# Layer 1's GLU spread to the end of the layer, with its buffers kept, and the routing's tables in weight buffers

## The chip, the cores and the metric

The kernel runs on one core of a Trainium2 chip. The metric is the device time of one execution in microseconds (us), the median of several runs. TensorE (PE) does the matmuls, VectorE (DVE) and ScalarE (ACT) the elementwise work, GpSimd (POOL) gathers and some elementwise work, and SyncE (SP) issues most of the DMAs. All of them run their own instruction queue in order and wait for each other by semaphores.

## The reference, cut to what matters

Four layers work on a residual stream `x` of 4 sequences of 512 tokens, width 256, all in float32. In each layer a normalized copy `xn` goes through an attention-like part and a feed-forward part, and both results are added to `x`:

```python
xn = layernorm(x)
x = x + attn_i(xn) + ffn_i(xn)
```

Layer 0 is a Mamba-2 mixer with a GLU. Layer 1 is the layer that the change touches first:

```python
# attention with low-rank queries and keys (16 heads, causal), 512 tokens a sequence
q  = rmsnorm(x @ wq_a) @ wq_b          # 192 -> 16 heads of 128 + 64 (rotary)
kv = rmsnorm((x @ wkv_a)[:, :64]) @ wkv_b
out = softmax(q k^T * scale, causal) v @ wo
# feed-forward: a GLU of width 1024, plus product-key experts
mlp = silu(x @ gate_w) * (x @ up_w) @ down_w
experts = sum over 8 of 512 experts, chosen by two top-8 searches, of silu(x . down_e) * softmax * up_e
```

Layer 2 has a small head-mixing attention, and a feed-forward part with 8 experts of which each token takes the best 2, plus a shared GLU of width 256:

```python
scores = softmax(x @ gate_w)                      # 2048 tokens x 8 experts
topk_w, topk_i = top_k(scores, 2)
y = sum over the 2 of w_e * (silu(x @ wg_e) * (x @ wu_e)) @ wd_e
shared = silu(x @ sg) * (x @ su) @ sd
```

Layer 3 has a full attention of 16 heads and 8 experts with a top-p rule.

## The kernel before

**Tiling.** Tokens are split into 16 tiles of 128 and 4 sequences of 512. `x` (tokens on partitions) and `xnT` (the normalized stream, transposed) stay in SBUF. When every stream of a layer has added its part for a sequence b, `part_done(b)` calls `layernorm(b)` for the next layer, which also writes the normalized tokens to DRAM.

**Weaving.** Inside a layer several Python generators ("streams") issue their work in turn. `weave` gives each stream a total cost and a start, and always advances the one whose place, start plus work done over its total, is lowest:

```python
live = [[start * total, total, gen] for gen, total, start in streams]
s = min(live, key=lambda s: s[0] / s[1])
cost = next(s[2], None)
```

The totals only set how far a stream spreads over the layer: a stream with a total above the sum of its costs ends early. This order is handed to a planner, which places the instructions on each engine's queue and assigns the buffers of each pool. Buffers of one tag are handed out in the order of the program. A pool that is opened over the memory of a closed one waits until all tiles there are done with.

**Layer 1's streams** (`layer1`, lines 1073 to 1104):

- `latent_pieces`: the attention, for 4 groups of 4 heads, 4 sequences and 2 pairs of heads: 32 pairs. For each head, score products (line 655), row maximum on DVE (658), exponential on ACT (662), scaling (775), transposes on PE (782) with copies out (786); for each pair of heads the value product (918, result `zT`), for each two pairs the output product (932) which is added to `x` (158). Queries (739 to 742) are made one pair ahead; half of their rows are turned by a copy from SBUF to SBUF on SP's queue (`psw`, 747). Each group takes a new weight block (713, 714, 721).
- `product_key_pieces`: two searches, then for each of the 16 token tiles 8 gathers on POOL (1036), 8 dot products on DVE (1046) and 8 additions (152).
- `glu_units`: the GLU in two halves of 512 hidden columns. The first half of sequences 0 and 1 is done in layer 0 already. For each half and sequence, four hidden blocks (two projections by line 134 of 512 columns each, tanh on ACT at 165, two DVE operations at 166 and 167, cost 3.4), then two steps of the down product (line 212, two token tiles each, cost 3.44) with an addition to `x` (158).
- `room`: starts at 0.915. It closes the right side's pools, loads layer 2's weights on POOL's queue (1589, 1591) and runs the routing of layer 2 for the first two sequences (`Half.dispatch`): router, softmax, comparison tables `before` and `tie` (1306 to 1310), ranks, counts, places, one-hot tables (1422), and a product of them (1430) that gives the ids of the tokens in each slot of the experts.

**Memory.** Pools with `side="right"` grow from the top of SBUF down, the others from the bottom up. Before, `p_keep`, `p_t` (product keys) and `g1` (the GLU: five `hT` of 2 KB and two `sg` of 2 KB a partition) are on the right, and `room` closes all three to place `t_keep` (25 KB) and `t_route` (14 KB) there. `t_route` holds the routing's tables: `before` in four buffers of 2 KB, and `sel`, `cum`, `pick`, `hit` and small ones. A separate pool `weights` has three buffers of 12 KB with the tag `wu`; every block of weights (`Ctx.unit`) takes the next that is free. In layer 1 the blocks are, in order: the attention's small weights, GLU half 0, attention groups 0 and 1, GLU half 1, attention groups 2 and 3; then layer 2's shared GLU (`t_shared`) and layer 3's four blocks (`f_units`).

**Layer 2** (`Layer2.run`) opens its pools on the right below `t_route`, gathers the tokens for the experts of the first half (`gather`, 1465), runs the second half's routing, the shared GLU, the head mixing and the experts (1495, 1517).

Of the kernel before, what the change touches and what calls it, by code (L numbers as in the profile page):

```python
# [15 lines left out]
P = 128  # L16
# [13 lines left out]
class Ctx:  # L30
# [12 lines left out]
    def tile(self, pool, shape, tag, dtype=F32, **kw):  # L43
        self.n += 1
        return pool.tile(shape, dtype, tag=tag, name=f"{tag}_{self.n}", **kw)
# [37 lines left out]
def v3(ap, b):  # L83
    return ap.rearrange("p (a b) -> p a b", b=b)
# [54 lines left out]
def project_tokens(c, out, w, cols, tokens):  # L139

    for d in range(2):
        c.nc.tensor.matmul(  # L142
            out, lhsT=c.xnT[:, d, tokens], rhs=w[:, d, cols], start=(d == 0), stop=(d == 1)
        )
# [81 lines left out]
def weave(c, *streams, flush=True):  # L226

    live = [[start * total, total, gen] for gen, total, start in streams]  # L230
    while live:
        s = min(live, key=lambda s: s[0] / s[1])
        cost = next(s[2], None)
        if cost is None:
            live.remove(s)
        else:
            s[0] += cost
        c.step()
    if flush:
        c.step(True)  # L240
# [833 lines left out]
def layer1(c, a, xn, following):  # L1074


    with ExitStack() as stack, ExitStack() as right:
        def pool_of(name, bufs, stack=stack, **kw):
            return stack.enter_context(c.tc.tile_pool(name=name, bufs=bufs, **kw))

        p_keep, p_t, glu = (pool_of(name, 1, right, side="right") for name in ("p_keep", "p_t", "g1"))
        dram = pool_of("p_dram", 1, space=bass.MemoryType.DRAM)
        keep = pool_of("l_keep", 1)
        latent = latent_pieces(c, a, keep, lambda: pool_of("l_h", 2))

        def glu_units():
            same = dict(tanh=True, bufs=5)
            yield from glu_pieces(c, glu, [a["g1_units"][0]], last=False, seqs=[2, 3], **same)
            yield from glu_pieces(c, glu, [a["g1_units"][1]], first=1, **same)

        def room():
            right.close()
            following.first()
            yield 1.0
            yield from following.routing(0)

        weave(
            c,
            (latent, 457.0, 0.0),
            (product_key_pieces(c, a, p_keep, p_t, dram, xn), 237.0, 0.02),  # L1100
            (glu_units(), 145.0, 0.0),
            (room(), 270.0, 0.915),
            flush=False,
        )
# [164 lines left out]
def softmax(c, s, m, scale):  # L1269

    nc = c.nc
    wide = list(s.shape)
    nc.vector.tensor_reduce(m, s, AX.X, ALU.max)
    nc.vector.tensor_sub(s, s, m[:, :, None].to_broadcast(wide))
    nc.scalar.activation(s, s, AF.Exp, scale=scale)
    nc.vector.tensor_reduce(m, s, AX.X, ALU.add)
    nc.vector.reciprocal(m, m)
    nc.vector.tensor_mul(s, s, m[:, :, None].to_broadcast(wide))


def router(c, pool, wr, bs, p=None, wide=1):

    nc = c.nc
    E, n = 8, len(bs) * TPB
    pl = c.ps()[:, : n * E]
    for i, b in enumerate(bs):
        c.settle(b)
        for t in range(TPB):  # L1290
            tt, to = b * TPB + t, (i * TPB + t) * E
            project_tokens(
                c, pl[:, to : to + E], wr, slice(0, E), slice(tt * P, (tt + 1) * P)
            )
    yield 2.0
    if p is None:
        p = c.tile(pool, [P, TPB, E], "p")
    nc.vector.tensor_copy(p, v3(pl, E))
    m = c.tile(pool, [P, n], "m")
    softmax(c, p, m, 1.0)  # L1300
    yield 2.0
    full = [P, n, E, E]
    other, own = p[:, :, None, :].to_broadcast(full), p[:, :, :, None].to_broadcast(full)
    before = c.tile(pool, full, "before", bufs=wide)
    tie = c.tile(pool, full, "before" if wide > 1 else "tie", bufs=wide)
    nc.vector.tensor_tensor(before, other, own, ALU.is_gt)
    nc.vector.tensor_tensor(tie, other, own, ALU.is_equal)
    low = v3(c.low, E)[:, None, :, :].to_broadcast(full)
    nc.vector.tensor_mul(tie, tie, low)
    nc.vector.tensor_add(before, before, tie)  # L1310
    return p, m, before, other
# [7 lines left out]
class Half:  # L1319
# [13 lines left out]

    def dispatch(self):
        c, k, pool, nc = self.c, self.k, self.pool, self.c.nc
        tile = lambda shape, tag, **kw: c.tile(pool, shape, tag, **kw)
        p, rank = tile([P, HT, E8], "p_half"), tile([P, HT, E8], "rank")
        before = yield from router(c, pool, k["router"], [2 * self.hf, 2 * self.hf + 1], p, 4)
        yield 2.0
        nc.vector.tensor_reduce(rank, before[2], AX.X, ALU.add)  # L1340

        both = [P, 2, HT, E8]
        sel = tile(both, "sel")
# [4 lines left out]
        cum = tile([P, 4, Z + HT, E8], "cum")  # L1348
# [10 lines left out]
        flat = lambda v: v.rearrange("p t e -> p (t e)")  # L1359
        pc = c.ps()  # L1360
        n = HT * E8
# [10 lines left out]
        full = [P, E8, E8]  # L1372
# [16 lines left out]
        pick = tile(both, "pick")  # L1389
# [11 lines left out]
        hit = tile(by_tile, "hit")  # L1401
# [16 lines left out]
        ats = []  # L1418
        four = [P, 4, P]
        for i in range(2 * HT // 4):  # L1420
            ats.append(tile(four, "before", bufs=4))
            nc.vector.tensor_tensor(
                ats[i], k["iota"][:, None, :].to_broadcast(four),
                part[:, 4 * i : 4 * i + 4][:, :, None].to_broadcast(four), ALU.is_equal,
            )
            yield 1.0
# [203 lines left out]
def top_p_experts(c, a):  # L1630
    nc, tc = c.nc, c.tc
    with tc.tile_pool(name="o_t", bufs=1, side="right") as pool:
        wr = c.tile(pool, [P, 16], "wr")
        nc.sync.dma_start(wr, a["o_router"])
        cws = c.tile(pool, [P, NTILE, 8], "cw")
        for b in range(NB):
            p, _, before, other = yield from router(c, pool, v3(wr, 8), [b])
            nc.vector.tensor_mul(before, before, other)
            cw = cws[:, b * TPB : (b + 1) * TPB, :]
            nc.vector.tensor_reduce(cw, before, AX.X, ALU.add)  # L1640
            nc.vector.scalar_tensor_tensor(
                cw, cw, float(np.float32(0.9)), p, ALU.is_le, ALU.mult
            )
            yield 1.0
        yield from glu_pieces(
            c, pool, [a["o_units"][e] for e in range(8)], factor=lambda e, t: cws[:, t, e : e + 1]
        )
# [17 lines left out]
def program(tc, a, x_in, out):  # L1665
    nc = tc.nc
    with ExitStack() as stack:
# [18 lines left out]
        c.parts(3, lambda b: layernorm(c, b, halves[b // 2][b % 2 * SEQ : (b % 2 + 1) * SEQ, :]))  # L1686
        second = Layer2(c, a, halves)
        layer1(c, a, c.xn, second)
        c.parts(3, lambda b: layernorm(c, b))
        c.pinned = True  # L1690
# [12 lines left out]
def rows(w):  # L1703

    k = w.shape[0] // P
    return w.reshape(k, P, -1).transpose(1, 0, 2).reshape(P, -1)
# [33 lines left out]
def glu_units(gate, up, down):  # L1740

    return np.stack([
        np.concatenate([rows(gate[:, s]), rows(up[:, s]), rows(down[s])], axis=1)
        for s in (slice(k, k + 512) for k in range(0, gate.shape[1], 512))
    ])
# [110 lines left out]
```

## Time and profile before

| what | us |
|---|---|
| median of 5 runs | 3129.32 |
| lowest and highest run | 3127.09, 3137.24 |
| the profiled execution | 3127.98 |
| its span, first to last instruction | 3126.2 |
| TensorE busy in the span | 3073.1 |
| VectorE, ScalarE, GpSimd busy | 1816.7, 1258.1, 650.4 |

All times inside the execution are counted from the start of the span. In the profile a line such as `PE mm L134 x8` names the engine, the tile that is written, the line of the kernel and the number of instructions; a float32 matmul of the program stands there as two instructions. `[3.35 <-PE mm L1430]` behind an instruction is the time that its engine stood before it, and what ended that. Layer 1 begins near 816 us and its attention ends near 1519 us.

### The profile page before, as it was taken

What the parts mean: (1) busy time and instruction counts of PE and PEld (TensorE: products, weight loads), DVE (VectorE), ACT (ScalarE), POOL (GpSimd) and SP (SyncE); (2) the same over time, 40 slices, a digit from 0 to 9 for tenths busy, and PEclk for the clock granted to TensorE, in tenths of its full rate; (3) what the DMA queues carried; (4) which work ended last, traced back from release to release, by engine and by line L of the source; (5) the groups of instructions that cost most, each with busy time, mean ns of one, the idle gap of its engine ahead of it and who ended that gap; (6) DMA issues with size and microseconds to landing.
All of it is one profiled execution on the core that took longest, in us unless ns stands there. A gap on an engine that the chain in (4) does not pass through costs nothing.

```text
span 3126.2 us, 35680 instructions
## 1 busy us (share of the span) xinstructions
PE 3073.1 (98%) x12502; PEld 1885.3 (60%) x12502; DVE 1816.7 (58%) x4644; ACT 1258.1 (40%) x2916; POOL 650.4 (21%) x517
## 2 busy tenths in 40 slices
PE   9999999999899999999999999999999999999999
PEld 5566566566655555555776656656566655555555
DVE  5777778777777787877656545455555422222222
ACT  4434435444466666667425433333333311111111
POOL 0465555556300133331242000000000000000000
PEclk9999999999999999999899999999999999999999
DMA  3233333233221154543242000000000000000000
GB/s 124 86 101 122 100 92 112 85 125 86 89 60 53 45 129 96 130 120 116 67 115 83 1 21 8 1 28 1 21 1 1 21 21 21 21 21 21 0 0 27
DMA packets 89090, 185.12 MB, mean 59 GB/s; under 512 B 14192, under 2 KB 57216, under 8 KB 84176
## 3 DMA queue, kind: packets, MB, share of 16 engines
q1 hardware_dynamic: 74448, 135.05, 13.6%
q0 software_dynamic: 14176, 47.01, 6.5%
q8 instruction: 99, 1.62, 0.2%
q10 hardware_dynamic: 288, 0.79, 0.1%
q14 instruction: 79, 0.65, 0.1%
HBM read 160.92 MB, written 12.98 MB: 56 GB/s over the span
## 4 chain that ended last, share of the span: by engine, by line
PE 88%; DVE 6%; POOL 2%; ACT 2%; DMA 1%; issue 1%; SPq 0%; ACTq 0%; DVEq 0%; POOLq 0%
PE mm L134 34%; PE acc L212 9%; PE mm L655 8%; PE mm L142 5%; PE acc L1165 4%; PE acc L671 4%; PE tr L509 3%; PE tr L1157 2%; PE tr L782 2%; PE tr L212 2%; PE acc L918 2%; PE acc L932 2%; PE acc L488 1%; PE mm L1495 1%; PE mm L478 1%; PE mm L741 1%
## 5 line engine op out<-in xcount | busy, mean ns | idle before, releaser
L134 PE MATMUL mm<-xnT,wu 128*128 128x512 f32 x2128 | 951.6, 595 | 0.2
L134 PEld LDWEIGHTS mm<-xnT,wu 128*128 128x128 f32 x2128 | 400.6, 191 | 462.0 <-issue 438.6
L662 ACT ACTIVATE pr<-pr,nm 128x128 f32<-128x128 f32 (+3 forms) x512 | 285.7, 558 | 293.6 <-DVE nm L658 291.2
L202 DVE TENSOR_TENSOR hT<-sg,mm 128x512 f32<-128x512 f32 x176 | 120.4, 684 | 393.8 <-PE mm L134 388.7
L201 ACT ACTIVATE sg<-mm 128x512 f32<-128x512 f32 x176 | 104.6, 595 | 580.0 <-PE mm L134 579.8
L658 DVE CUSTOM_DVE_ANT_0 pr<-mm,late 128x128 f32<-128x128 f32 (+3 forms) x512 | 245.3, 482 | 92.0 <-PE mm L655 89.4
L212 PE MATMUL acc<-wu,hT 128*128 128x256 f32 x1280 | 287.1, 380 | 1.7 <-DVE x L158 1.7
L212 PEld LDWEIGHTS acc<-wu,hT 128*128 128x128 f32 x1280 | 241.4, 190 | 49.9 <-issue 17.2
L1036 POOL DMA_INDIRECT e<-in_p_experts,ids x128 | 130.4, 1018 | 477.0 <-DVE x L152 354.0
L134 PE MATMUL mm<-xnT,w_in 128*128 128x512 f32 x512 | 228.5, 593 | 0.1
L280 DVE SCALAR_TENSOR_TENSOR cy<-mm,ws,cy 128x509 f32<-128x509 f32 (+2 forms) x216 | 159.7, 745 | 65.4 <-ACT cy L276 61.8
L655 PE MATMUL mm<-kf,qf 128*128 128x128 f32 (+3 forms) x512 | 179.6, 451 | 2.0 <-DVE nm L658 1.3
L655 PE MATMUL mm<-k,q 128*128 128x128 f32 (+3 forms) x512 | 176.5, 434 | 1.0 <-DVE q L1130 1.0
L449 POOL TENSOR_TENSOR G<-G,CB 128x1024 f32<-128x1024 f32 x64 | 152.8, 2388 | 92.5 <-DVE G L415 92.5
L435 ACT ACTIVATE xD<-xc,ws 128x128 f32<-128x128 f32 x256 | 84.1, 391 | 195.9 <-POOL y L472 186.3
L134 PEld LDWEIGHTS mm<-xnT,w_in 128*128 128x128 f32 x512 | 96.7, 190 | 107.9 <-issue 101.2
L152 DVE SCALAR_TENSOR_TENSOR x<-acc,cw,x 128x256 f32<-128x256 f32 x128 | 61.9, 483 | 153.7 <-PE acc L212 153.6
L1165 PE MATMUL acc<-PT,V 128*128 128x512 f32 (+3 forms) x512 | 149.1, 433 | 0.0
L415 DVE TENSOR_TENSOR_SCAN G<-G,eye 128x1024 f32<-128x1024 f32 x64 | 146.8, 2295 | 0.0
L1130 DVE TENSOR_SCALAR q<-mm,bias 128x512 f32<-128x512 f32 x64 | 48.0, 750 | 165.3 <-PE mm L134 165.3
L782 PEld LDWEIGHTS tr<-con,pr 128*128 128x128 f32 x640 | 81.2, 143 | 88.7 <-ACT pr L775 27.4
L142 PE MATMUL mm<-wu,xnT 128*128 128x512 f32 (+1 forms) x320 | 129.2, 551 | 2.3 <-DVE sg L166 2.3
(337 smaller groups left out, 4925.7 us busy)
## 6 DMA issues: line engine op xcount, KB each, us to landing
G<-own SPq DMA_DIRECT2D x64, 512.0 KB, 4.3
w_in<-in_m_units SPq DMA_DIRECT2D x16, 1024.0 KB, 5.3
eb<-since SPq DMA_DIRECT2D x96, 128.0 KB, 3.5
wu<-in_o_units SPq DMA_DIRECT2D x8, 1536.0 KB, 6.5
wo<-in_m_units SPq DMA_DIRECT2D x16, 512.0 KB, 4.2
psw<-pes SPq DMA_DIRECT2D x128, 64.0 KB, 3.1
wu<-in_g_units SPq DMA_DIRECT2D x4, 1536.0 KB, 7.0
wu<-in_f_units SPq DMA_DIRECT2D x4, 1536.0 KB, 7.2
```

Of the source, the lines that this page charges most:

```text
L134: c.nc.tensor.matmul(out, lhsT=w[:, d, cols], rhs=c.xnT[:, d, tokens], start=(d == 0), stop=(d == 1))
L142: c.nc.tensor.matmul(out, lhsT=c.xnT[:, d, tokens], rhs=w[:, d, cols], start=(d == 0), stop=(d == 1))
L212: nc.tensor.matmul(po[:, j, :], lhsT=hT[k][:, (t + j) * P : (t + j + 1) * P], rhs=wd[:, k, :], start=(i == 0), stop=(i == per - 1),)
L280: nc.vector.scalar_tensor_tensor(y[:, j:], src[:, : SEQ - j], conv[:, k, 3 - j : 4 - j], y[:, j:], ALU.mult, ALU.add,)
L415: tc.keep_in_program_order(nc.vector.tensor_tensor_scan(flat, flat, eye.rearrange("p h t -> p (h t)"), 0.0, ALU.mult, ALU.add))
L449: nc.gpsimd.tensor_mul(G, G, seqs[b][2][:, t, :][:, None, :].to_broadcast([P, HG, P]))
L655: nc.tensor.matmul(sc, lhsT=q[:, i * P : n], rhs=k[:, :n], start=True, stop=True)
L658: nc.vector.tensor_tensor_reduce(out=pr, in0=sc, in1=late[:, SEQ - n :], scale=1.0, scalar=-NEG, op0=ALU.add, op1=ALU.min, accum_out=nm,)
L662: nc.scalar.activation(pr, pr, AF.Exp, bias=nm, scale=-1.0, accum_out=total)
L782: nc.tensor.transpose(pt[:, (i - j) * P : (i - j + 1) * P], prs[s][i][:, j * P : (j + 1) * P], c.ident)
L1036: nc.gpsimd.indirect_dma_start(out=e, out_offset=None, in_=a["p_experts"], in_offset=bass.IndirectOffsetOnAxis(ap=ids[:, t, k : k + 1], ax ...
L1165: nc.tensor.matmul(z[:, j * P :], lhsT=head["V"][:, j, h, :], rhs=head["PT"][:, j, j * P :], start=(j == 0), stop=(j == TPB - 1),)
```

## The change

Three edits belong together. The GLU's pool `g1` moves to the left side, as the first pool there, so that closing the right side no longer ends it; its total in the weave falls from 145 to 126, so that its last pieces are issued later in the layer. The tables `before`, `tie`, `sel`, `cum`, `pick` and `hit` of a routing, and the four one-hot tables, no longer have tiles in `t_route`: each routing takes one 12 KB buffer of the `wu` tag and cuts them out of it (columns 0 to 2047 for the 512-wide tables, the rest behind). The `wu` tag thus has two more takers: the first routing between attention group 3 and `t_shared`, the second between `t_shared` and layer 3's first block. The `room` argument of `router` is left out in layer 3, where the tables stay in that layer's pool.

```diff
--- before.py
+++ after.py
@@ -1078,7 +1078,8 @@
         def pool_of(name, bufs, stack=stack, **kw):
             return stack.enter_context(c.tc.tile_pool(name=name, bufs=bufs, **kw))
 
-        p_keep, p_t, glu = (pool_of(name, 1, right, side="right") for name in ("p_keep", "p_t", "g1"))
+        p_keep, p_t = (pool_of(name, 1, right, side="right") for name in ("p_keep", "p_t"))
+        glu = pool_of("g1", 1)
         dram = pool_of("p_dram", 1, space=bass.MemoryType.DRAM)
         keep = pool_of("l_keep", 1)
         latent = latent_pieces(c, a, keep, lambda: pool_of("l_h", 2))
@@ -1098,7 +1099,7 @@
             c,
             (latent, 457.0, 0.0),
             (product_key_pieces(c, a, p_keep, p_t, dram, xn), 237.0, 0.02),
-            (glu_units(), 145.0, 0.0),
+            (glu_units(), 126.0, 0.0),
             (room(), 270.0, 0.915),
             flush=False,
         )
@@ -1278,8 +1279,7 @@
     nc.vector.tensor_mul(s, s, m[:, :, None].to_broadcast(wide))
 
 
-def router(c, pool, wr, bs, p=None, wide=1):
-
+def router(c, pool, wr, bs, p=None, room=None):
 
 
     nc = c.nc
@@ -1301,8 +1301,12 @@
     yield 2.0
     full = [P, n, E, E]
     other, own = p[:, :, None, :].to_broadcast(full), p[:, :, :, None].to_broadcast(full)
-    before = c.tile(pool, full, "before", bufs=wide)
-    tie = c.tile(pool, full, "before" if wide > 1 else "tie", bufs=wide)
+    if room is None:
+        before, tie = c.tile(pool, full, "before"), c.tile(pool, full, "tie")
+    else:
+        before, tie = (
+            v.rearrange("p (t e f) -> p t e f", e=E, f=E) for v in (room[:, :512], room[:, 512:1024])
+        )
     nc.vector.tensor_tensor(before, other, own, ALU.is_gt)
     nc.vector.tensor_tensor(tie, other, own, ALU.is_equal)
     low = v3(c.low, E)[:, None, :, :].to_broadcast(full)
@@ -1333,9 +1337,22 @@
 
     def dispatch(self):
         c, k, pool, nc = self.c, self.k, self.pool, self.c.nc
-        tile = lambda shape, tag, **kw: c.tile(pool, shape, tag, **kw)
+
+        room = c.tile(c.weights, [P, 3072], "wu")
+        ends_at = [2048]
+
+        def tile(shape, tag):
+            if tag not in ("sel", "cum", "pick", "hit"):
+                return c.tile(pool, shape, tag)
+            n = int(np.prod(shape[1:]))
+            flat = room[:, ends_at[0] : ends_at[0] + n]
+            ends_at[0] += n
+            if len(shape) == 3:
+                return v3(flat, shape[2])
+            return flat.rearrange("p (a b c) -> p a b c", b=shape[2], c=shape[3])
+
         p, rank = tile([P, HT, E8], "p_half"), tile([P, HT, E8], "rank")
-        before = yield from router(c, pool, k["router"], [2 * self.hf, 2 * self.hf + 1], p, 4)
+        before = yield from router(c, pool, k["router"], [2 * self.hf, 2 * self.hf + 1], p, room)
         yield 2.0
         nc.vector.tensor_reduce(rank, before[2], AX.X, ALU.add)
 
@@ -1418,7 +1435,7 @@
         ats = []
         four = [P, 4, P]
         for i in range(2 * HT // 4):
-            ats.append(tile(four, "before", bufs=4))
+            ats.append(v3(room[:, i * 512 : (i + 1) * 512], P))
             nc.vector.tensor_tensor(
                 ats[i], k["iota"][:, None, :].to_broadcast(four),
                 part[:, 4 * i : 4 * i + 4][:, :, None].to_broadcast(four), ALU.is_equal,
```

## Prediction

> **What bounds the kernel now.** I read the page first. TensorE is busy in 98% of the span and no other engine in more than 58%; slices 14 to 20 of its table hold layer 1's attention.
>
> ```profile
> PE 3073.1 (98%) x12502; PEld 1885.3 (60%) x12502; DVE 1816.7 (58%) x4644; ACT 1258.1 (40%) x2916; POOL 650.4 (21%) x517
> PEclk9999999999999999999899999999999999999999
> ```
>
> Then the chain of waits, for the places of two things in layer 1: the value product of a pair of heads (line 918, 32 of them), which marks the pace of the attention, and the pieces of the GLU. A piece is a hidden block (eight matmuls of 512 columns, line 134) or two token tiles of the down product (sixteen of 256 columns, line 212).
>
> ```profile
> 1326.68 3.44 PE mm L134 x8
> 1376.79 3.46 PE acc L212 x16
> 1381.21 2.30 PE acc L918 x16
> 1392.46 3.65 PE acc L212 x16
> ...
> 1459.01 2.30 PE acc L918 x14
> 1496.10 2.54 PE acc L918 x14
> ```
>
> A piece costs TensorE 3.44 to 3.65 us, and the last one ends at 1396. Next the windows from every second value product to the next (a double step: two pairs of heads of one sequence and their output product). Columns: length, busy time and count of PE, weight loads, DVE, ACT, POOL, granted clock, DMA share, GB/s.
>
> ```profile
> 1223.10:1260.10 37.00, 36.97 (x153) 20.24 (x152) 29.48 (x100) 25.45 (x68) 12.24 (x13) 1.00 0.58 116
> 1260.10:1300.60 40.50, 40.46 (x179) 24.71 (x178) 32.33 (x106) 24.79 (x68) 15.91 (x16) 1.00 0.43 112
> 1340.60:1381.10 40.50, 39.78 (x169) 22.62 (x168) 33.38 (x110) 27.26 (x72) 14.08 (x15) 1.00 0.55 124
> 1381.10:1418.40 37.30, 37.28 (x170) 22.11 (x168) 30.20 (x108) 26.59 (x68) 9.05 (x9) 1.00 0.40 126
> 1418.40:1458.90 40.50, 37.52 (x175) 22.92 (x174) 30.90 (x110) 28.32 (x72) 8.08 (x9) 0.92 0.56 163
> 1458.90:1496.00 37.10, 32.03 (x146) 19.33 (x144) 27.56 (x97) 26.79 (x69) 0.00 (x0) 0.91 0.19 64
> ```
>
> They hold 2, 3, 3, 1, 0 and 0 pieces. Up to 1418 TensorE has no gap and another piece makes a double step longer. In the last two, without pieces, it stands 3.0 and 5.1 us and runs part of the time at a lower clock, yet they are no shorter: they wait for softmax, layernorm and the routing. So layer 1 has a front (to 1398) paced by TensorE and a tail (1398 to 1512) paced by waits such as these, the largest of TensorE between 1397 and 1545:
>
> ```profile
> PE tr L782 <- DVE PT L786: 2.7, 2, 1.7
> PE tr L782 <- ACT PT L786: 2.2, 3, 1.4
> ```
>
> **The change, part by part.** *The order.* A stream's place is its start plus work done over its total. The GLU's pieces cost 122.9 of a total of 145, so the last started at 0.824; with 126 it starts at 0.948. Laid over the attention's steps, the 15 double steps from 900 us held 3 2 3 2 2 3 2 3 2 3 2 3 1 0 0 pieces (TensorE's instructions in the trace agree) and will hold 2 2 2 2 2 2 2 3 2 2 2 2 2 2 2. Five pieces leave the front, one from each of five double steps, and five enter the last three: one, two and two.
>
> *Front, gain.* The starts of line 918 give the lengths 41.9 39.2 46.1 37.6 38.2 40.5 39.1 40.2 37.0 40.5 40.0 40.5 37.3 40.5 37.1. (The third, seventh and eleventh also hold the products of a new weight block.) Without these, three pieces take 40.7 on the mean and two take 38.0: 2.7 a piece. The extreme pair, 40.2 against 39.2, gives 1.0; a full piece of TensorE is 3.65. I take 3.2, between the mean and the full piece because PE has no gap there: 5 x 3.2 = 16 us, bounds 5 and 18.
>
> *Tail, loss.* Five pieces are 17.2 us of TensorE if nothing hides them. The double step at 1381 has no gap: its second piece costs 3.2. The two later ones have 3.0 + 5.1 = 8.1 us of gaps, and clocks of 0.92 and 0.91, which over 40.5 and 37.1 us are 3.2 + 3.3 = 6.6 us lost: 14.7 for four pieces of 13.8. Perfect filling would cost nothing; the gaps are short and the queue is in order, so I put 1.8 us on them. Tail: +5 us, bounds 3 and 17. With the pieces go three tanh of 0.6 us on ACT and 5.5 us on DVE (eight instructions of 0.69 us); DVE is idle for 9.6 of the 40.5 us and 9.5 of the 37.1, so they lie beside other work.
>
> A page of the Trainium skill speaks against this. The weight loads are busy for 285.71 of 497.50 us in the front and 64.58 of 114.10 in the tail, 57% both.
>
> ```profile
> 900.40:1397.90 497.50, 493.67 (x2163) 285.71 (x2162) 393.58 (x1344) 321.03 (x859) 111.93 (x110) 1.00 0.36 86
> 1397.90:1512.00 114.10, 105.46 (x487) 64.58 (x486) 83.25 (x299) 79.48 (x200) 11.44 (x12) 0.91 0.35 108
> ```
>
> "Perfetto Trace Analysis", section "Identifying the Most-Contended Engine", says that matmul busy time does not measure how full TensorE is and that the weight loads' share does; by that the front is no fuller than the tail, moving work between them brings nothing, and the sum is 0. I go by the lengths of the double steps.
>
> *The tables.* The same instructions write and read them. Their 12 KB buffer is that of the attention's third weight block, free since the load at 1310.40 below took it; the first table is written after 1465, so no wait: 0. But loads take buffers in program order, and these queue behind:
>
> ```profile
> 1310.40 0.34 SPq L53 DMA_DIRECT2D wu<-in_t_shared  x1
> 1396.14 0.34 SPq L53 DMA_DIRECT2D wu<-in_f_units  x1
> 1470.49 0.34 SPq L53 DMA_DIRECT2D wu<-in_f_units  x1
> ```
>
> Layer 2's shared weights must come after the tables' buffer, into the next one that is free, which is that of query 31: the place of the third load here, 1470.5. Ahead of and behind it on SP stand the same copies (psw, line 747, at 1471.1) that stand there now. Landing took 5.4 us, so 1476; their first matmul is at 1509: 33 us of cover, cost 0, and 1 us for each us that it is late. Layer 3's first block moves from 1396 to the second routing's tables (after 1530); its first matmul is at 1662, cover over 100 us. The second block needs the second tables' buffer, near 1590, and is used after 1850. All 0, bounds 0 and +3.
>
> *Memory.* The GLU's 14 KB move to the left side below the attention's, so its first tanh waits for the end of layer 0's additions (821.5) instead of its last product (816); in the trace that tanh starts at 821.5 anyway. 0, bounds 0 and +2. Layer 2's gathers still lie over the attention's buffers and wait for its last product:
>
> ```profile
> 1519.38 1.00 POOL L1465 DMA_INDIRECT xs<-xn_half,ids  x1 [76.63 <-DVE mv L103]
> ```
>
> The routing's ids are there at 1505.3, so the routing may slip by 14 us before the experts do. Layer 3's mask (line 643), for which DVE stands 2.85 us at 1512 to 1515, finds its place free earlier: gain 0 to 2.85; I take 0, since the next DVE work waits for ACT until 1517.
>
> *Sum.* -16 + 5 = -11 us. The profiled execution took 3127.98 us (span 3126.2 and 1.8 around it), so 3117.0 there; it lies 1.3 under the median of 3129.32, so 3118.3.
>
> **The rivals.** *Slower: the tail is a chain, and the pieces stand in its way.* PE's queue is in order. A piece ahead of a score product (line 655) delays the maximum on DVE, the exponential on ACT and the transposes; when it is done, the next wait is as long as before. Then the five cost 17.2, and with a front at its low rows (5) the sum is +12: 3141. The waits named above speak for it, the gaps' number against. It decides from the point where the tail gives back less than the front saves.
>
> *Nothing: the front is not TensorE's.* Its DVE is busy 79% and each engine waits in order. At the lower rows it saves 5 to 8, the tail takes 5: 3127 to 3129. Or the front saves 16 and the tail takes 17: 3130. Against the first speaks that PE has no gap there.
>
> *It does not do what it says.* The planner could order TensorE otherwise; the agreement of all 15 counts speaks against that. 3129.
>
> **How the numbers follow.** The forecast, with 3111 to 3122, has 0.69: 0.64 of it below 3119.9 and 0.05 above. Nothing 0.14, at 3125 to 3133; not as it says 0.02; slower 0.15, at 3139 to 3145. About 0.3% (9.4 us) is what a measurement can tell from no change: faster 0.64, same 0.21, slower 0.15. The range 3109 to 3134 leaves out the slower case and a little at the lower end.
>
> **What would show it.** Right: the double steps that lose a piece shrink to 37 or 38 us; the last piece stands near 1465; in the last two double steps PE's gaps and the low clock fade while their length stays within 2 us; the shared weights' load stands near 1460 and nothing waits for it. Wrong: those two grow by 6 or more, or a first table, shared matmul or psw copy waits for a weight buffer.

## The result, and the profile after

The changed kernel took 3132.92 us, median of 27 runs (3120.35 to 3140.16); the kernel before took 3131.58 beside it (50 runs). The ratio is 1.000, 95% interval 0.9993 to 1.0007: no change, where 3118.3 was forecast. The profiled execution of the changed kernel took 3140.17 us (span 3138.4), longer than each of the 27, so its parts are compared from layer 1's own start. Behind layer 1's last value product both profiled executions took the same (1614.2 us before, 1614.1 after).

The starts of the value products (line 918) stand in the trace of after at 1226.2, 1263.4, 1301.1, 1350.3, 1388.6, 1427.1, 1469.6 and 1508.4 for every second pair. Between them, as in the prediction, columns: length, busy time and count of PE, weight loads, DVE, ACT, POOL, granted clock, DMA share, GB/s:

```profile
1226.20:1263.40 37.20, 37.20 (x172) 22.98 (x170) 28.59 (x99) 22.80 (x61) 11.89 (x13) 1.00 0.58 118
1263.40:1301.10 37.70, 36.24 (x155) 19.68 (x154) 30.85 (x103) 24.90 (x69) 14.16 (x15) 1.00 0.41 103
1301.10:1350.30 49.20, 46.86 (x177) 24.24 (x176) 32.55 (x111) 27.20 (x71) 11.43 (x12) 0.86 0.37 80
1350.30:1388.60 38.30, 37.11 (x171) 22.26 (x170) 29.69 (x99) 24.57 (x66) 14.46 (x15) 1.00 0.49 119
1388.60:1427.10 38.50, 38.20 (x167) 20.79 (x167) 33.32 (x119) 28.93 (x75) 9.00 (x10) 1.00 0.35 94
1427.10:1469.60 42.50, 42.15 (x193) 24.89 (x192) 33.53 (x114) 30.25 (x78) 8.36 (x9) 0.97 0.56 154
1469.60:1508.40 38.80, 37.96 (x177) 23.85 (x176) 30.41 (x107) 25.38 (x65) 0.00 (x0) 0.99 0.14 45
```

Rows 2 and 4 were 40.5 us before and lost a piece: 37.7 and 38.3. The last three were 37.3, 40.5 and 37.1 and took in one, two and two pieces: 38.5, 42.5, 38.8, with PE's gaps and the low clock all but gone. All this was forecast. The third row was not: it kept its two pieces and went from 40.0 to 49.2, with 2.3 us of gaps and a clock of 0.86.

For the whole layer I use three marks: its first latent product (line 142), the 25th value product and the last. Front is from the first to the second, tail from the second to the third. Two rows of windows of before, then two of after:

```profile
813.50:1381.10 567.60, 557.53 (x2418) 324.98 (x2417) 441.49 (x1514) 367.50 (x995) 119.46 (x130) 1.00 0.35 86
1381.10:1512.00 130.90, 122.26 (x564) 74.67 (x562) 96.77 (x342) 90.01 (x228) 17.13 (x18) 0.92 0.34 105
```

```profile
821.90:1388.60 566.70, 551.83 (x2372) 316.32 (x2371) 431.34 (x1498) 363.98 (x987) 118.85 (x130) 0.99 0.34 84
1388.60:1524.30 135.70, 133.64 (x613) 80.11 (x612) 104.38 (x362) 92.84 (x237) 17.36 (x18) 0.96 0.31 88
```

Length less PE's busy time is its idle time; half of the time at which the trace's clock record stands at 0.5 is lost to the half clock; busy time less that loss is TensorE's work. Front: 567.6 to 566.7 us, of which work 557.5 to 545.0 (551.83 less 6.8), idle 10.1 to 14.9, half-clock loss 0 to 6.8. Tail: 130.9 to 135.7, of which work 112.1 to 128.6, idle 8.6 to 2.1, loss 10.2 to 5.1. So the tail went as forecast (+4.8 for +5), and the front, from which 16 us were to come, gave 0.9. In the sum of both, **idle plus loss was 28.9 us before and is 28.8 after**: the change carried idle time and half clock from the tail into the front.

The waits of PE, first in the tail of after, then in its front from 900 us on, with DVE's for the copy psw there (us in total, times, longest):

```profile
PE tr L782 <- ACT PT L786: 0.6, 1, 0.6
```

```profile
PE mm L655 <- DVE qf L759: 4.3, 3, 2.0
PE acc L932 <- ACT zT L924: 1.5, 1, 1.5
DVE psw L757 <- DMA psw<-pes: 12.9, 7, 3.2
```

The tail's waits named in the prediction (2.7 and 2.2 us) have shrunk to 0.3 and 0.6. The front has new ones of PE for the rotated queries (qf); from 900 us to its end the front of before had none of these. DVE's wait for psw is no new one: it was 10.5 us in 7 times there before. The chain of waits shows the longest, and the windows what comes behind it:

```profile
1301.56 4.69 DMA psw<-pes
...
1306.44 0.69 DVE psw L757
```

```profile
1309.90:1323.60 13.70, 13.36 (x22) 5.14 (x22) 6.16 (x26) 6.84 (x18) 1.05 (x1) 0.50 0.12 30
```

The swapped copy lands at 1306.3; DVE stands 2.25 us for it, PE 1.97 us for DVE, and 1.1 us later PE runs 13.7 us at half clock although it is busy for 13.36 of them. In the trace of before a down product (line 212, 3.7 us) stands there behind the same queries, and PE doesn't wait. The shared weights' load is at 1482.49 (near 1460 in the forecast), nothing waits for it, and layer 2's gathers still follow the last value product.

```profile
1482.49 0.34 SPq L53 DMA_DIRECT2D wu<-in_t_shared  x1
```

One thing was not forecast: the first write to the new tables (a memset of `cum`, line 1366) stands in DVE's queue at 1316.6, not after 1465, and DVE stood 3.2 us there, until the query product that still read this weight buffer was done. PE was busy meanwhile.

### The profile page after: what moved, and what is told of

Same layout as the page of the kernel before. It is cut to its first block, busy times and chain, and to the rows that moved or that the text cites. A ratio compares the mean times of both kernels' runs of the same rounds, so it can differ in the third digit from the quotient of the medians.

```text
span 3138.4 us, 35693 instructions
## 1 busy us (share of the span) xinstructions
PE 3087.2 (98%) x12502; PEld 1887.8 (60%) x12502; DVE 1813.5 (58%) x4644; ACT 1257.4 (40%) x2916; POOL 649.4 (21%) x517
## 4 chain that ended last, share of the span: by engine, by line
PE 85%; DVE 8%; POOL 2%; ACT 2%; DMA 2%; issue 1%; SPq 0%; ACTq 0%; DVEq 0%; POOLq 0%
PE mm L134 33%; PE acc L212 9%; PE mm L655 7%; PE mm L142 5%; PE acc L1166 4%; PE acc L671 4%; PE tr L509 3%; PE tr L1158 2%; PE tr L782 2%; PE tr L212 2%; PE acc L918 2%; PE acc L488 1%; PE mm L1512 1%; PE acc L932 1%; DMA psw<-pes 1%
## 5 line engine op out<-in xcount | busy, mean ns | idle before, releaser
L212 PEld LDWEIGHTS acc<-wu,hT 128*128 128x128 f32 x1280 | 240.8, 190 | 46.9 <-issue 17.1
L509 PE MATMUL tr<-wo,y 128*128 128x256 f32 x512 | 126.6, 390 | 4.9 <-DVE acc L515 4.9
```

Of the source, the lines that this page charges most:

```text
L212: nc.tensor.matmul(po[:, j, :], lhsT=hT[k][:, (t + j) * P : (t + j + 1) * P], rhs=wd[:, k, :], start=(i == 0), stop=(i == per - 1),)
L509: nc.tensor.matmul(po, lhsT=y[:, k, :], rhs=groups[i][1][:, k, :], start=(k == 0), stop=(k == 3))
```

## The experiments

Runs e1 to e8 come from jobs in which the kernel before took 3195 to 3197 us, e9 to e18 from jobs in which it took 3132 to 3136; ratios are always to the kernel before in the same job. Columns: ratio with its 95% interval, then from the one profiled run layer 1's length (front plus tail), its parts, and how many of the 32 pairs of 64-row products (lines 741 and 742, see e14) are neighbours on PE.

| run | ratio | length | work | idle | half-clock loss | neighbours |
|---|---|---|---|---|---|---|
| before | | 698.5 | 669.6 | 18.7 | 10.2 | 11 |
| after | 1.000 (0.9993-1.0007) | 702.4 | 673.6 | 16.9 | 11.9 | 13 |
| e1 before again | 1.0009 (1.0000-1.0018) | 713.0 | 671.8 | 29.2 | 11.9 | 11 |
| e2 after again | 1.0001 (0.9989-1.0012) | 715.9 | 674.5 | 29.4 | 11.9 | 13 |
| e3 buffers alone | 0.9983 (0.9972-0.9994) | 709.6 | 672.1 | 27.3 | 10.2 | 11 |
| e12 the same again | 0.9987 (0.9975-0.9999) | 692.6 | 671.9 | 17.3 | 3.4 | 11 |
| e13 tables alone | 0.9993 (0.9982-1.0004) | 694.6 | 670.5 | 17.3 | 6.8 | 11 |
| e4 rotation later | 1.0002 (0.9990-1.0014) | 709.1 | 673.6 | 28.7 | 6.8 | 14 |
| e7 copy earlier | 1.0018 (1.0008-1.0028) | 717.6 | 676.9 | 30.5 | 10.2 | 10 |
| e8 the same in before | 1.0013 (1.0002-1.0024) | 716.1 | 677.7 | 28.1 | 10.2 | 8 |
| e5 after less 5 pieces | 0.9966 (0.9956-0.9976) | 702.5 | 660.4 | 31.8 | 10.2 | 12 |
| e16 the same again | 0.9995 (0.9985-1.0006) | 693.6 | 658.2 | 25.2 | 10.2 | 12 |
| e6 before less 5 pieces | 0.9965 (0.9952-0.9978) | 705.6 | 654.1 | 32.7 | 18.8 | 10 |
| e11 shifted | 0.9984 (0.9973-0.9994) | 689.2 | 670.1 | 14.3 | 4.8 | 9 |
| e9 piece after queries | 0.9994 (0.9980-1.0008) | 694.7 | 675.1 | 14.5 | 5.1 | 6 |
| e10 piece after rotation | 0.9956 (0.9940-0.9972) | 678.3 | 663.7 | 13.3 | 1.3 | 17 |
| e17 the same again | 0.9950 (0.9930-0.9969) | 680.7 | 664.0 | 15.0 | 1.7 | 17 |
| e18 one step later | 0.9930 (0.9912-0.9948) | 677.3 | 656.8 | 18.7 | 1.7 | 30 |
| e14 paired products | 0.9977 (0.9967-0.9987) | 686.4 | 657.3 | 22.3 | 6.8 | 32 |
| e15 paired, as e10 | 0.9974 (0.9962-0.9985) | 687.5 | 656.5 | 25.9 | 5.1 | 31 |

A single profiled run is no mean. From after to e10, for instance, the length falls by 24 us and the ratio says 14; where the two differ, the ratio decides.

**e1, e2: both kernels again.**

> The kernel before, unchanged, beside itself, for its own granted clock, waits and scatter on this chip. Theory A (the front's gain is real and is given back: the tail grows by 5.8 us, and the swapped copy of the rotary queries, psw of line 747, now holds DVE's rotation of line 757 and then TensorE's scores): the double steps between 916.8 and 1397.9 us repeat within 1 us each, 'DVE psw L757 <- DMA psw' stays near 10 us, and PE waits for the rotation's qf less than 1 us in all. Theory B (what differs between the two traces is mostly where the half-clock stretches fall, which changes from run to run): the value products move by 3 to 8 us between this trace and the first one of the same kernel, at steps that hold a stretch. Ratio 1.000 within 0.001 in both.

> The changed kernel, unchanged. Theory A: the psw wait repeats (16 us of DVE, 4 us of PE in layer 1's front, at the same pairs), the first double step is again 47 to 50 us long, and layer 1 from its first latent product to its end takes about the same as before, within 3 us. Theory B: the 13.7 us half-clock stretch at 1310 and the 49.2 us double step are not there again, and layer 1's front is 5 to 8 us shorter than in the first trace of this kernel. Ratio against the kernel before: 1.000 in theory A; in theory B 0.998 to 1.000.

The first double steps repeat to 0.1 us (41.9 in before, 49.4 in after), and so does PE's wait for qf near 1309 (2.08 us, near 1310). The half-clock stretch behind it is 3.4 us in e2 instead of 13.7; it varies, the wait doesn't. Front, e1 to e2: 577.4 to 573.3; tail 135.5 to 142.6. Idle plus loss is 41.1 and 41.3: unchanged again. Both theories were half right: new waits in the front repeat, the clock's cost scatters, and the ratio is 1.

**e3, e12, e13: the buffers without the spreading.** In e3 and e12 `(glu_units(), 145.0, 0.0)` is put back in the changed kernel; e13 also puts `g1` back on the right, so that only the tables move.

> The changed kernel with the GLU's total put back to 145: the moved buffers and tables alone, the pieces where they were. Theory A: the move costs nothing, ratio 1.000, double steps as before. Theory C (the move of the GLU's buffers costs at layer 1's start, where the first double step grew from 41.9 to 49.4 us, or the tables' buffer holds a load back): 6 to 10 us slower, ratio 1.002 to 1.003, and the first double step is again 48 us or more. Then the spreading alone is worth about -8 us.

> The changed buffers with the GLU's total at 145 once more, since it came out at 0.9983. If the move of the buffers is worth something (layer 2 or the routing starts earlier): 0.997 to 0.999 again, and the stretch from the last value product to the end 1 us or more shorter. If the two kernels are the same but for scatter: 0.9990 to 1.0010.

> The kernel before with the routing's tables in the spare weight buffer, and nothing else changed: the GLU's buffers stay on the right side and its total at 145. If the -4.7 us of e3 and e12 come from the tables (a free buffer lets the routing's first instructions be ordered otherwise in the last two pairs, so that the rotation there no longer stands in front of a score maximum): 0.9980 to 0.9990, and the last three value products 5 to 6 us closer together than before (47 to 48 us from the 29th to the last, against 53). If they come from the GLU's buffers: 0.9995 to 1.0008, and 53 us.

The move alone is worth 0.15% (two runs agree), 4.7 us *faster*; the first double step is 42.6, so its growth to 49.4 belongs to the spreading (the stretch ahead of it, from the first mark to the first value product, shrank from 86.9 to 76.4 us, so the two together lost 2.9). Front and tail of e12:

```profile
814.60:1382.80 568.20, 558.23 (x2418) 324.66 (x2417) 442.09 (x1516) 366.83 (x995) 118.42 (x130) 1.00 0.33 85
1382.80:1507.20 124.40, 117.12 (x563) 70.79 (x562) 96.64 (x343) 89.48 (x228) 16.92 (x18) 0.97 0.31 92
```

Against these buffers the spreading makes the tail 11.3 us longer (124.4 to 135.7) and the front only 1.5 shorter, and idle plus loss rises from 20.7 to 28.8 us; from e3 to e2 the tail grows by 11.4 (131.2 to 142.6), the front gives 5.1, and idle plus loss goes from 37.5 to 41.3. The last of the three windows of e13 (29th to 31st value product, no piece in it) is 33.1 us; before it was 37.1 with 5.1 us of gaps:

```profile
1468.00:1501.10 33.10, 29.74 (x145) 17.26 (x144) 28.89 (x105) 26.52 (x69) 0.00 (x0) 1.00 0.15 49
```

So the tables do this part, in all three runs (33.2, 33.2, 33.1). In before the rotation and a row maximum follow each other on DVE, and PE waits for both (DVE's rows, then PE's):

```profile
1482.63 0.69 DVE L759 TENSOR_TENSOR qf<-pec,psw 64x512 f32<-64x512 f32 x1
1483.49 0.42 DVE L658 CUSTOM_DVE_ANT_0 pr<-mm,late 128x256 f32<-128x256 f32 x1
```

```profile
1483.97 0.49 PE L655 MATMUL mm<-kf,qf 128*128 128x128 f32 x2 [1.26 <-DVE nm L658]
1486.16 0.47 PE L782 MATMUL tr<-con,pr 128*128 128x128 f32 x1 [1.70 <-DVE PT L786]
```

In e12 the rotation is done at 1478.65, ahead of that maximum; the same score product doesn't wait, and the one behind it waits 0.22 us. The order in the engines' queues came out otherwise with the tables elsewhere. e13's ratio, 0.9993, is too close to both expectations to share the 4.7 us out between tables and GLU buffers; that stays open.

**e4, e7, e8: is it the copy psw?** In e4 the rotation is issued at step 2 of the odd query (`if i == 2 and s % 2 == 1`), in e7 the queries at step 0 of the even one (`if i == 0 and s % 2 == 0 and s < 62: turning = queries(...)`); e8 is the latter in the kernel before.

> The changed kernel with the rotation (line 757) issued two score steps later in the same odd query (step 2 instead of step 0), so that about 2.3 us more of PE's work covers the copy psw. Theory A: the wait of DVE for psw falls from 16 us to under 5, PE's wait for qf in the front from 4.3 to under 1, and the kernel is 4 to 8 us faster: ratio 0.9975 to 0.9987. Theory B: the waits fall likewise, the time stays within 2 us (ratio 0.9994 to 1.0006). A third way: the rotation now stands right ahead of the next pair's scores and PE waits for qf there instead, 1 to 2 us in each of 31 pairs: slower by 10 us or more.

> The changed kernel with the queries' products and the copy psw issued one score step earlier (step 0 of the even query instead of step 1), the rotation where it was: the copy gets 1.1 us more of cover, and the scores wait no later than now. Theory W (what the front's gain was given back to is the psw wait and the half-clock stretches after it): DVE's wait for psw falls under 6 us, PE's for qf under 1, the stretch at 1310 goes, 5 to 8 us faster than the changed kernel, ratio 0.9975 to 0.9985. Theory M: the waits move on to the transposes (line 782) and the score maxima, ratio 0.9993 to 1.0007.

> The same edit in the kernel before. Theory W: its PE waits for no qf in the front, so nothing to take: within 2 us, ratio 0.9994 to 1.0006, and 4 us or more behind the changed kernel with the same edit. Theory M: both within 2 us of the kernel before and of one another.

PE's wait for qf in the front fell from 4.1 us (e2) to 1.7 in e4 and to nothing in e7; DVE's for psw stayed in e4 (8.5 us in e2, 8.7) and fell to 3.0 in e7. The time didn't follow: 1.0002 and 1.0018. In e7 the transposes wait 8.3 us for ScalarE's copies of PT (in e2 5.0 us for DVE's), and 4.8 us go to zT (2.4 in e2). Theory W falls: the psw wait is where the front's idle time showed, not why it is there. Take it away and the idle time stands elsewhere. e7 and e8 are even slower than theory M has it (at most 1.0007 and 1.0006); TensorE's work rose by 2.4 us from e2 to e7 and by 5.9 from e1 to e8, with three pairs of neighbours fewer in each.

**e5, e16, e6: the price of five pieces.** The last five pieces are not computed (e5, e16 from the tail of after; e6 from the front of before).

```diff
+            out5 = tanh and last and b == NB - 1
             for k in range(n):
+                if out5 and k > 0:
+                    yield 3.4
+                    continue
...
```

> The changed kernel without the GLU's last five pieces (three hidden blocks and both down products of the last sequence's second unit, 17.4 us of TensorE, all in the tail): that part is left out of the result, all other pieces stand where the change puts them. The time against the kernel before is then the front's gain alone, and against the changed kernel the tail's price alone. The forecast's sum: 16 us faster than before, ratio 0.995. Theory M (waits and half-clock stretches appear in the front where the pieces left, so the front gives 4 to 9 us and the tail takes 5 to 7): 4 to 9 us faster, ratio 0.9972 to 0.9987, with PE's gaps in the front at 10 us or more and at 8 or more in the tail.

> The kernel before without the same five pieces (left out of the result); there they are the last of the front, from about 1325 to 1396 us. The forecast's sum: a piece in the front costs 3.2 us, so 16 us faster, ratio 0.995, and the double steps that had three or two pieces shrink to 33 to 34 us. Theory M: a double step has a floor of some 37 us that waits set, so those that fall to one or no piece hardly shrink: 5 to 9 us faster, ratio 0.997 to 0.9984, and PE's gaps in the front grow by 5 us or more.

> The changed kernel without its last five pieces (left out of the result) once more. e5 gave 0.9966 against 1.000 for the changed kernel: 11 us for five pieces in the tail. If that holds: 0.9955 to 0.9975. The forecast's tail (+5) would show as 0.9980 to 0.9988.

Pieces of some 17 us are gone (the layer's work falls by 14.1 us from e2 to e5 and by 15.4 from after to e16); e5 against e2 gives 11 us (0.9966 against 1.0001), e16 against after only 2 (0.9995 against 1.000). The two don't agree within their intervals, so by the ratios the tail's price is not settled closer than 0 to 16 us; e16 lies outside both ranges expected for it. The traces say why it is never 17: the tail shrinks by 4.5 us (135.7 to 131.2, e16) and 10.3 (142.6 to 132.3, e5), while its idle plus loss grows by 10.8 and 4.8. In e6 the front shrank by 15.3 us (577.4 to 562.1), which is the forecast's price for a front piece, but the tail grew by 8.0 without any piece more (idle 12.6 to 19.7, loss 11.9 to 17.1), and the ratio is again 11 us, not 16.

**e11, e9, e10, e17, e18: the same density, another place in the pair.** e11 starts the GLU's stream at 0.0136. The others issue four pieces ahead and then one in each pair of heads:

```diff
+            if i == 2 and s % 2 == 1 and s < 64:
+                next(piece, None)
+                yield 0.0
...
-            (glu_units(), 126.0, 0.0),
+            (first_four(), 150.0, 0.0),
```

(e10 and e17 as shown, after the rotation; e9 behind the queries, `i == 1 and s % 2 == 0`; e18 at `i == 3`.)

> The changed kernel with the GLU's stream begun half a spacing later (start 0.0136 of the layer in place of 0): the same density, every piece 1.7 units later, the last one near 0.962. Theory P: the waits for psw and zT change by 5 us or more, either way, and the time with them. Theory M and equal prices for front and tail: ratio 1.000 within 0.0012, S to the last value product within 4 us of the changed kernel's 716.

> The changed kernel's buffers, with the GLU's pieces tied to the attention: four before it, then one in each pair of heads, right behind the queries' products, so that each piece (3.4 us of TensorE) covers the copy psw. The density is the change's (two in each double step), only the place in the pair is fixed. Theory P (the front's gain was lost since pieces at a drifting place in the pair leave the copy and the transposes uncovered): DVE's wait for psw under 4 us, PE's for qf 0, no half-clock stretch in the front, 5 to 9 us faster than before, ratio 0.9972 to 0.9985. Theory M (a piece covers one wait and uncovers another; the sum of gaps and of half-clock losses in the layer stays at 25 to 40 us): ratio 0.9992 to 1.0015.

> The same with the piece half a pair later (behind step 2 of the odd query, after the rotation): the psw copy is covered by no piece in any pair. Theory P: DVE's wait for psw grows to 30 us or more and PE's for qf to 10 or more, 8 to 20 us slower than the kernel with the piece after the queries, ratio to before 1.001 to 1.005. Theory M: within 4 us of it.

> e10 once more. If its gain is real (TensorE's work 664 us, gaps and half-clock time 15 us in layer 1): 0.994 to 0.9975. If it was scatter: 0.9985 to 1.000, with gaps and half-clock time at 22 us or more.

> e10 with the piece one step later (step 3 of the odd query, the last before the next pair); 30 of 32 pairs of the 64-row products are neighbours there, against 17 in e10 and 13 in the changed kernel. If TensorE's work sets the time: 12 us less work than e10, 0.991 to 0.993. If the sum of work, gaps and half-clock time sets it and the missing work comes back as in e14 and e15: 0.995 to 0.9985, with gaps and half-clock time 8 us or more over e10's 15.

The place decides. e9, which has a piece behind every copy (DVE's wait for psw from 900 us on is 7.4 us, against 15.9 in after), gains nothing by its ratio (0.9994). Front and tail of e11:

```profile
814.30:1368.10 553.80, 542.50 (x2370) 314.52 (x2369) 429.31 (x1498) 365.87 (x991) 117.68 (x130) 1.00 0.34 87
1368.10:1503.40 135.30, 132.35 (x605) 80.13 (x604) 104.08 (x361) 92.07 (x232) 17.07 (x18) 0.96 0.31 85
```

Against e12 (same buffers, old spread) the front does give 14.4 us here, near the forecast's 16, with 11.3 us of gaps and no half clock. But the tail takes 10.9, and the ratios of the two (0.9984, 0.9987) are the same. Theory P's mechanism is wrong, though: it held the copy psw to be what a piece must cover, and e10 covers it in no pair. It is 14 us faster than before, though DVE stands longer for psw in its front (15.8 us, and 22.9 in e18, against 12.9 in after); PE's wait for qf is 0 in both. Front and tail of e10, then of e18, then DVE's wait in e18's front:

```profile
813.40:1359.10 545.70, 534.35 (x2356) 310.75 (x2355) 432.45 (x1496) 367.12 (x987) 116.86 (x130) 1.00 0.34 87
1359.10:1491.70 132.60, 130.67 (x621) 79.90 (x620) 105.30 (x364) 93.77 (x237) 17.31 (x18) 0.99 0.31 91
```

```profile
824.70:1369.00 544.30, 529.30 (x2354) 306.30 (x2354) 430.30 (x1494) 363.31 (x986) 118.43 (x130) 1.00 0.35 86
1369.00:1501.90 132.90, 129.18 (x623) 79.94 (x622) 105.96 (x364) 93.51 (x237) 16.93 (x18) 0.99 0.35 92
DVE psw L757 <- DMA psw<-pes: 22.9, 12, 3.3
```

e10's idle plus loss is 14.6 us (16.7 in e17), against 28.8 in after, 14 us less. Its work is 10 us less too, some 4 of them by four more pairs of neighbouring products. e18 has 17 us less work than after, some 15 of them, estimated at 0.9 us a pair, by 17 more such pairs, and 20.4 us of idle plus loss: 0.993, about 22 us faster than the kernel before. Both beat both kernels. So the gain of the place is partly gaps and clock and partly TensorE's work; why the gaps close at these places and not in e9's, no run shows.

**e14, e15: take TensorE's work out of the queries.**

```diff
-        nc.tensor.matmul(pe, lhsT=wpe1[:, cols], rhs=qa1[:KL, tokens], start=False, stop=True)
-        nc.tensor.matmul(pl, lhsT=wl1[KL:, cols], rhs=qa1[KL:, tokens], start=False, stop=True)
+        with tc.high_priority():
+            tc.keep_in_program_order(
+                nc.tensor.matmul(pe, lhsT=wpe1[:, cols], rhs=qa1[:KL, tokens], start=False, stop=True)
+            )
+            nc.tensor.matmul(pl, lhsT=wl1[KL:, cols], rhs=qa1[KL:, tokens], start=False, stop=True)
```

> The changed kernel with the two 64-row products of the queries (lines 741 and 742, on rows 0 to 63 and 64 to 127 of the array) issued one behind the other in all 32 pairs, by a higher priority for them; in the changed kernel 13 of the 32 are neighbours. In the traces neighbours start 0.01 us apart and take 0.52 us together, for each of two passes, others 0.43 to 0.53 each: 0.9 us a pair, 17 us for 19 more pairs. Theory T (the front is paced by TensorE's work, wherever the waits lie): 12 to 19 us faster than the changed kernel, ratio to before 0.994 to 0.996. Theory M (the attention's waits set a floor, so that time taken from TensorE comes back as gaps): 0 to 7 us, ratio 0.998 to 1.000, with PE's gaps 10 us up.

> The same edit in e10 (a piece in each pair behind the rotation), where 17 of 32 were neighbours: 14 more pairs by 0.9 us, 13 us. Theory T: 10 to 14 us faster than e10's 0.9956, ratio to before 0.991 to 0.9925. Theory M: 0 to 5 us, 0.994 to 0.996. It is also the version that should beat both kernels by most.

With the higher priority the two products stand next to each other in every pair of e14. The work fell by 16.3 us from after to e14 (17 expected) and by 7.2 from e10 to e15 (13 expected). The time fell by 7 us (0.9977) in the one and didn't fall in the other: it rose by some 6 (0.9974 against 0.9956 and 0.9950, intervals that overlap a little). Idle plus loss went from 14.6 to 31.0 us in e15. So theory T fails for both: time taken from TensorE need not shorten the layer, though TensorE is busy in 96 to 98% of its front. It isn't the opposite either: e18, expected at 0.991 to 0.993 if TensorE's work sets the time and at 0.995 to 0.9985 if the missing work comes back as gaps, came out at 0.9930, with only 6 us more idle and loss than e10.

## Why the prediction was wrong, by its own steps

**The order: right.** All 15 piece counts came out, and the double steps that lost a piece and lay in the middle of the layer shrank (46.1 to 42.7, 40.5 to 37.6, 37.7 and 38.3). The last piece starts at 1491, not near 1465: the attention stood 12.4 us later there than before (31st value product at 1508.4 against 1496.0), the rest is a later place in the order.

**Front, gain -16: the failed step.** It measured -0.9 in the profiled run and -4.1 from e1 to e2; e16 and e5, whose fronts hold what the changed kernel's holds, give -5.2 (against before) and -7.2 (against e1). Its reason was that PE has no gap there, so that each piece taken out brings its full 3.2 us. That holds while the other work stays packed, and here it didn't. Of 17.2 us of pieces, 12.5 show as less work, idle time grew by 4.8 and half-clock loss by 6.8 (from e1 to e2 14.5, 5.3 and 5.1). The five double steps that lose a piece, the first taken with the stretch ahead of it, did give 14.2 us; the other seven of the front took 13 of them back. The step looked only at the double steps that lose a piece and counted the others as fixed; 40.0 to 49.2 was one of those. Why the work fell by 12.5 and not 17.2 stays open; the trace shows where: the same 500 transposes (line 782) were busy for 94.0 us before and 97.9 after, the 32 products of line 714 for 8.2 and 9.7. That gaps need not open is shown by e11, where five pieces fewer, with all pieces at other places, brought 14.4.

**Tail, +5: right by balance of two errors.** It measured +4.8 against before. Against the same buffers it is 11.3 (e12), 11.4 (e3 to e2) and 10.9 (e11), twice the forecast, well inside its bounds of 3 and 17: the 1.8 us put on four pieces in the last two double steps was too little. So even with e11's front the sum stays near nothing. What hid this is the next step.

**Tables and memory, 0: wrong in sign.** The bounds were 0 to +5 us; e3 and e12 gave -4.7. The prediction named one gain (the mask at 1512, up to 2.85) and missed that moving tables can reorder DVE's queue: in the last two pairs, where it helped, and at 1316.6, where the first table did wait for its buffer.

**The sum.** Buffers -4.7, spreading +4.7 by the ratios (1.000 against 0.9983 and 0.9987): no change. In the terms above, the move left the work about as it was (669.6 and 673.6 us), so a gain had to come out of idle time and half clock. The forecast of -11 says in effect that their 28.9 us would fall to 18. It counted what the tail would lose of them and never asked what the front would gain.

**The rivals.** "Nothing" came out, by a third way: neither the front at its low rows with a cheap tail nor a full front with a full tail, but a front whose gaps opened and a tail at twice its price, paid for by the buffers. Its time, 3127 to 3130, was near. The rule of the Trainium skill ("Perfetto Trace Analysis", section "Identifying the Most-Contended Engine") gave a sum of 0 and met the result. The weight loads' share is now 316.32 of 566.70 us in the front and 80.11 of 135.70 in the tail, 56% and 59%. The same shares stand in e10 (57% and 60%), which is 14 us faster, so the share doesn't tell what a placement is worth.

**What would show it.** Most signs of "right" came, and the time didn't: four of the five double steps shrank, though the third only to 42.7, and the first of the five grew; in the last two the gaps and the low clock faded while their length stayed within 2 us; the last piece and the shared weights' load came 26 and 22 us late. Of the signs of "wrong" one came, the first table's wait of 3.2 us. The signs watched only the places that gained or lost a piece; the sum of idle time and half clock over the whole layer would have told.

## What to carry to other kernels

Before pricing a move of work between stages on one engine, split the stage's length into work, idle time and clock loss: a move leaves the first about as it is, unless other instructions come to stand side by side (e18's work is 17 us less), so its gain has to come out of the other two, and both ends must be asked. An engine that is busy 98% of a stage can still lose there what its filler work covered; here the filler's place in the cycle was worth more (14 to 22 us) than its density (nothing, or a loss of some 5 us against the same buffers). A wait that is taken away and comes back under another name was a symptom.

## What the runs showed of the hardware

**Two 64-row products run at once.** When the products of lines 741 (rows 0 to 63) and 742 (rows 64 to 127) stand next to each other on PE, they start 0.01 us apart and the next instruction starts 0.52 us after (at full clock; in one pair of e14's 32 they started 0.45 us apart even so); apart, each takes 0.52 or 0.53 us to the next start. First before, where transposes stand between them, then e18:

```profile
1292.73 0.59 PE L741 MATMUL mm<-qa,wu 64*128 64x512 f32 x1
1293.25 0.88 PE L782 MATMUL tr<-con,pr 128*128 128x128 f32 x6
1294.05 1.12 PE L742 MATMUL mm<-qa,wl 64*128 64x512 f32 x2
```

```profile
1024.69 0.69 PE L741 MATMUL mm<-qa,wu 64*128 64x512 f32 x1
1024.69 0.69 PE L742 MATMUL mm<-qa,wl 64*128 64x512 f32 x1
1025.22 0.59 PE L741 MATMUL mm<-qa,wu 64*128 64x512 f32 x1
```

The Trainium skill, "TensorE: Matmul & The Clock Gate", Part 3 on packing small matmuls, says that products on different row groups overlap with starts some 4 ns apart; the trace agrees, with 6 or 7 ns.

**The half clock comes in pieces of 3.4 us and behind short waits.** Stretches lasted 3.4, 6.8, 10.2, 13.7 and up to 27.3 us, and one of 13.7 followed a PE wait of 1.97 us while PE was busy. Behind the same wait a stretch of 3.4 us stands in e2, e4, e14 and e16, and none in e5. The same page's Part 1, in its table of the two states, puts the half clock behind an idle window of some 3.4 us; no single PE gap of after's front was that long (1.97 us at most). It scatters between runs of the same kernel: the stretch up to layer 1 took 821.9 us in after and 813.9 in e2, with 8.5 and 5.1 us of half-clock loss.

**Jobs differ.** The jobs of 3195 to 3197 us ran on chips 6 and 8, those of 3132 to 3136 on chips 5, 13 and 14. In the former the stretch behind layer 1 took 1665 us instead of 1614 to 1620, with 26 to 27 us of half-clock loss and 49 to 52 of idle time (2 to 8 and 7 to 11 in the latter), and ACT and DVE at times stood 4 us together with no releaser in the program's work; the cause is open.
